# Local attention in a five-block model: the value product with channels on the partitions, and the query norm inside the mask-and-maximum op

## The chip, the cores and the metric

The kernel runs on one core of one Trainium2 chip, as one program in fp32. The metric is device time in microseconds (us). Three runs of the kernel before gave 1146.81, 1147.2 and 1147.84, median 1147.2. Engine names: PE is the matmul engine (PEld its weight loads), DVE the vector engine, ACT the scalar engine, POOL the GpSimd engine, SP the queue that issues nearly all DMAs.

## The reference

The input is x of shape (4, 512, 128): 4 batches, 512 positions, 128 channels. Six blocks follow each other, each with a residual sum around a layer norm: a gated feed-forward, a 16-head attention with a position bias, the same feed-forward again, then twice a block of two local-attention layers with a recurrence between. What the change touches is the local attention, of which there are 2 blocks x 2 layers x 4 batches = 16 calls. Cut to what matters:

```python
qkv = h @ wqkv                       # 8 heads of 64 channels
q = l2norm(q) * qs ; k = l2norm(k) * ksc
q, k = rotary_xpos(q, k)             # q*cos*scale + rotate_half(q)*sin*scale, and so on
# windows of 64 queries; keys: the window before and the same window (128 keys)
sim = einsum('bhwid,bhwjd->bhwij', bq * 8.0, bk)
sim = where((i < j) | (i > j + 64) | (j == -1), -max, sim)
attn = softmax(sim)
out = einsum('bhwij,bhwjd->bhwid', attn, bv)
x = x + out @ wo
x = x + feed_forward(x)              # layer norm, 128 -> 2*341, a * gelu(g), -> 128
```

## The kernel before

**A planner writes the order.** The kernel does not issue instructions as its functions run. Each call on an engine is recorded as an `Op` with a guessed cost and a due time (`plan.vt`); `Plan.plan` (lines 179 to 265) then places the ops one by one, as each engine comes free and its inputs and buffers are there, the one with the earliest due time first; `emit` issues them in that order and `pin` fixes it, so that every engine works through one fixed list. All instructions therefore carry line 318, where the recorder calls the engine. Costs, due-time steps (`STEP`, `TURN`), and a few biases are constants at the head of the file. Buffers are slots that the planner hands out: 8 PSUM banks "psS", 33 "pair" buffers of which each can serve as two "half" ones, 24 "small" tiles, 8 "va" tiles for values.

**Stages.** The first feed-forward and the 16-head attention (head pair by head pair, batch by batch) fill the first 420 us or so; the feed-forward again overlaps with its end; the local blocks follow, the four batches shifted against each other and interleaved by the planner. From the first to the last product with `wqkv` it is 423 to 1075 us.

**One call of `local_attention` (lines 684 to 875)** treats 4 tiles of 128 positions, so there are 64 tiles in all. A tile passes these functions, several steps apart (`behind`, line 869), while other tiles and other batches are between them:

- `rotate` (690): two products with `wqkv` for q and k; ACT squares them; DVE multiplies by the cos and sin tables into `u` and `w`; POOL adds halves of the squares, DVE sums them, three small ACT ops give the inverse norms `rn` of 8 query and 8 key heads; POOL adds the rotated halves and multiplies all 1024 columns of `u` by `rn` (line 721).
- `values` (726): the product for v, copied by ACT into `va` of 8 x 65 columns; column 64 of each head holds ones, so that the value product also gives the softmax sum.
- `turn` (734): 4 PE transposes turn the queries, ACT copies them; the keys are turned by a DVE block transpose and DMAs.
- `soften` (771): 16 small products give scores for 8 heads x 128 keys. One DVE op per head (lines 790 to 794) adds the mask, negates, writes the result and its minimum `mx`. ACT takes exp of the first 4 heads with `mx` as bias; for the other 4 heads POOL subtracts `mx` (line 798) and ACT takes one exp.
- `turn_back` (804): 8 PE transposes turn the undivided exponentials, ACT copies them to `pT`; DMAs bring the values of the window before into `vm`.
- `weigh` (822): the value product with positions on the partitions: 16 products, weights `pT` (64 columns of positions), moving `val` (65 columns). DVE takes the reciprocal of the sums (line 838) and multiplies 4 heads at a time out of PSUM (line 839).
- `turn_outputs` (844): 4 PE transposes bring channels onto the partitions, ACT copies.
- `project` (853): 4 products with `wo`, two DVE adds into the residual `h`.

Of the kernel before, what the change touches and what calls it, by code (L numbers as in the profile page):

```python
# [9 lines left out]
ALU = mybir.AluOpType  # L10
# [25 lines left out]
KEYS = 2 * WIN  # L36
DX = DH + 1
QK_SCALE = 8.0
NEG = -1.0e30

# [13 lines left out]
PAIRS = 33  # L54
STEP, TURN = 3.368, 10.272
ATTN, LATE, LAG, LATER = 28.945, 383.972, 3.899, 11.219

# [63 lines left out]
class Plan:  # L121
# [3 lines left out]

    LATENCY, HORIZON, SWITCH, TABLE = 0.07, 52.328, 0.1, 1.28
    IDLE, COLD, FIRST = 2.5, 8.0, 6

    TAIL = {"tensor": 0.16, "vector": 0.085, "scalar": 0.115, "gpsimd": 0.05}
    MODE_BIAS, TABLE_BIAS = 15.205, 15.629  # L130

# [167 lines left out]
class Recorder:  # L299
# [36 lines left out]
    def cost(self, name, outs, ins, kw, n):  # L336

        if name == "dma_start":
            return 0.55
        if name == "matmul":  # L340
            return max(0.22, ins[1].size() / 597.0)
        if name == "transpose":
            return 0.12 if self.engine == "tensor" else 0.62
        if n is None:
            n = max(v.size() for v in (ins if name == "tensor_reduce" else outs) or outs)
        if self.engine == "vector":
            if name == "tensor_tensor_scan":
                return 1.2
            psum = any(v.tile.kind == "S" for v in ins)
            lo, hi = (outs + ins)[0].region()[0]  # L350
            if name == "tensor_tensor_reduce":
                return 0.078 + 0.00104 * n
            inside = len(ins) > 1 and n > 256 and not psum
            return 0.064 + 0.00104 * n + 0.09 * (hi - lo <= 64) + 0.06 * (len(ins) > 2) + 0.3 * inside
        if self.engine == "scalar":
            if name == "copy":
                return 0.04 + 0.00083 * n
            wide = len(ins) > 1 or any(v.tile.kind != "S" for v in ins)
            return 0.05 + 0.00083 * n + 0.09 * wide + 0.06 * ("accum_out" in kw)
        if name == "memset":  # L360
            return 0.1 + 0.0008 * n
        return 0.145 + 0.0022 * n
# [66 lines left out]
def tile_macaron(ctx: ExitStack, tc: tile.TileContext, i: dict, out: bass.AP):  # L429
# [6 lines left out]
    def real(name, shape, pool=pool):  # L436
# [4 lines left out]
            "S": [real(f"psS{n}", [P, T], psum) for n in range(8)],  # L441
            "small": [real(f"small{n}", [P, 2 * H1]) for n in range(24)],
            "va": [real(f"va{n}", [P, H1, DX]) for n in range(8)],
            "via": [real(f"via{n}", [P, 2 * T], dram) for n in range(8)],
# [239 lines left out]
    def local_attention(l, h):  # L684
        wqkv, wo = wqkv_sb[l], wo1_sb[l]
        cs, sn = cos_sb[l], sin_sb[l]
        half = DH // 2
        us, qTs, kTs, vas, vms, es, pTs, os_, oTs = ({} for _ in range(9))

        def rotate(t):  # L690
# [27 lines left out]
            for lo, hi in ((slice(0, half), slice(half, DH)), (slice(half, DH), slice(0, half))):  # L718
                pool_.tensor_tensor(u4[..., lo], u4[..., lo], w4[..., hi], ALU.add, n=INNER)
            u3 = u.rearrange("p (h d) -> p h d", d=DH)  # L720
            pool_.tensor_tensor(
                u3, u3, rn.unsqueeze(2).to_broadcast([P, 2 * H1, DH]), ALU.mult, cost=1.87
            )
            us[t] = u

        def values(t):
# [3 lines left out]
            )  # L730
            va = vas[t] = plan.tile("va", [P, H1, DX])
            act.copy(va[:, :, :DH], pv)

# [37 lines left out]
        def soften(t):  # L771
# [26 lines left out]
            pool_.tensor_tensor(  # L798
                rest, rest, mx[:, BIASED:].unsqueeze(2).to_broadcast([P, H1 - BIASED, KEYS]), ALU.subtract
            )  # L800
            act.activation(rest, rest, AF.Exp, scale=-1.0)
            es[t] = e

        def turn_back(t):


            vm = vms[t] = plan.tile("half", [P, H1, DX])
            dma.dma_start(out=vm[64:128], in_=vas[t][0:64])
# [252 lines left out]
    w_h = cload("w_h", [D, D], i["L1_attn_Wh"])  # L1061
    for va in memory.slots["va"]:
        pool_.memset(plan.fixed(va, [P, H1, DX])[:, :, DH:], 1.0)


# [13 lines left out]
def _constants():  # L1079
# [92 lines left out]
```

## Time and profile before

| what | value |
|---|---|
| median of three runs | 1147.2 us |
| the profiled execution: span from first to last instruction | 1146.1 us |
| median less span (what lies around it) | 1.1 us |
| granted PE clock | 1.00 of full speed |
| instructions: PE, DVE, ACT, POOL | 9036, 2891, 1948, 575 |
| local blocks | from about 420 us to the end |
| PE transposes in all | 1488 that read a "pair" buffer, 1024 of them in the local attention |

How to read it: the page gives busy time of each engine and a strip of 40 slices with busy tenths; a busy PE is one that has a matmul in its pipeline. Further views give the chain of work that ended last, groups of instructions of one shape with count, busy time and mean duration, busy time by stretches of time, and a timeline. A group's mean duration is from an instruction's start to its end; consecutive instructions on PE, DVE and ACT overlap, so that what one costs its engine is the distance from start to start, which the timeline tells. An fp32 product of PE is recorded as two instructions, a transpose as one.

### The profile page before, as it was taken

How to read it: one execution, taken by the hardware profiler on the slowest of the kernel's cores; microseconds unless marked ns; L12 is line 12 of the kernel's file. 1: busy time of each engine (PE TensorE's matmuls, PEld its weight loads, DVE VectorE, ACT ScalarE, POOL GpSimd, SP SyncE). 2: the span in 40 equal slices, each digit the busy share in tenths (PEclk: the TensorE clock that was granted, in tenths of full speed). 3: DMA queues.
4: the chain of work that ended last, by engine and by line, in shares of the span. 5: the costliest groups of instructions: out<-in, count | busy, mean ns of one | idle time of the engine just before them, and what ended most of it. 6: DMA issues, size and time to landing. Idle time of an engine off the chain costs nothing.

```text
span 1146.1 us, 26884 instructions
## 1 busy us (share of the span) xinstructions
PE 1117.0 (97%) x9036; PEld 688.4 (60%) x9036; DVE 911.9 (80%) x2891; ACT 877.0 (77%) x1948; POOL 762.7 (67%) x575
## 2 busy tenths in 40 slices
PE   7999999999999999999999999999999999999997
PEld 3455656566655545557667666764457766666673
DVE  4787787868778779989788788867999978878863
ACT  5987777867787667878786788788887777777764
POOL 3675655656569459979776677523999867777610
PEclk9999999999999999999999999999999999999999
DMA  4379799797979744523432332300333423322310
GB/s 126 125 232 306 211 261 264 207 274 206 299 211 309 199 115 127 161 84 106 120 96 68 93 102 76 85 1 1 98 114 102 115 77 101 98 84 67 98 38 19
DMA packets 131613, 157.01 MB, mean 137 GB/s; under 512 B 15034, under 2 KB 101732, under 8 KB 131476
## 3 DMA queue, kind: packets, MB, share of 16 engines
q1 hardware_dynamic: 131188, 155.21, 46.4%
q8 instruction: 73, 1.20, 0.5%
q14 instruction: 64, 0.52, 0.2%
q10 hardware_dynamic: 288, 0.08, 0.0%
HBM read 78.39 MB, written 64.02 MB: 124 GB/s over the span
## 4 chain that ended last, share of the span: by engine, by line
PE 70%; DVE 13%; ACT 9%; issue 3%; POOL 2%; DMA 1%; SPq 0%; DVEq 0%; ACTq 0%; POOLq 0%
PE psS L318 70%; DVE pair L318 12%; ACT pair L318 7%; POOL pair L318 2%; DVE small L318 1%; ACT small L318 1%; DMA pair<-via 1%; ACT L288 1%; ACT va L318 1%; SPq L318 0%; DMA via<-pair 0%; DMA pair<-in_x_dram 0%; DVE xT L318 0%; DVEq L318 0%; ACTq L318 0%
## 5 line engine op out<-in xcount | busy, mean ns | idle before, releaser
L318 POOL TENSOR_TENSOR pair<-pair,small 128x1024 f32<-128x1024 f32 (+1 forms) x256 | 430.9, 1704 | 203.6 <-DVE small L318 127.7
L318 PE MATMUL psS<-pair,pair 64*64 64x128 f32 (+4 forms) x4544 | 372.5, 300 | 3.2 <-DVE small L318 1.3
L318 ACT ACTIVATE pair<-pair,small 128x128 f32<-128x128 f32 (+1 forms) x512 | 266.5, 553 | 91.7 <-DVE small L318 77.1
L318 PEld LDWEIGHTS psS<-pair,pair 128*64 128x64 f32 (+2 forms) x4544 | 252.6, 140 | 101.5 <-issue 31.3
L318 ACT COPY pair<-psS 128x512 f32<-128x512 f32 (+1 forms) x470 | 254.6, 593 | 63.5 <-PE psS L318 59.0
L318 POOL TENSOR_TENSOR pair<-pair,pair 128x512 f32<-128x512 f32 x166 | 215.2, 1309 | 109.1 <-ACT pair L318 66.8
L318 PEld LDWEIGHTS psS<-ident,pair 128*128 128x128 f32 x1488 | 171.2, 141 | 92.5 <-issue 69.9
L318 PE MATMUL psS<-ident,pair 128*128 128x128 f32 x1488 | 200.0, 275 | 9.2 <-DMA pair<-in_x_dram 5.5
L318 DVE CUSTOM_DVE_ANT_0 pair<-psS,pair 128x512 f32<-128x512 f32 x256 | 164.8, 679 | 37.1 <-PE psS L318 36.3
L318 PE MATMUL psS<-wqkv,pair 128*128 128x512 f32 x384 | 182.2, 598 | 3.4 <-DVE pair L318 3.0
L318 DVE STREAM_TRANSPOSE pair<-pair 128x512 f32<-128x512 f32 x208 | 142.8, 697 | 18.9 <-POOL pair L318 18.0
L318 POOL TENSOR_TENSOR pair<-pair 128x512 f32<-128x512 f32 x82 | 102.9, 1256 | 55.8 <-ACT pair L318 54.7
L318 PE MATMUL psS<-pair,w 128*128 128x512 f32 (+2 forms) x288 | 130.2, 595 | 0.4 <-POOL pair L318 0.2
L318 ACT ACTIVATE pair<-pair 128x512 f32<-128x512 f32 x152 | 94.5, 629 | 35.6 <-DVE pair L318 26.4
L318 DVE CUSTOM_DVE_ANT_0 pair<-psS,mask 128x128 f32<-128x128 f32 x512 | 113.9, 284 | 6.2 <-PE psS L318 4.8
L318 PE MATMUL psS<-pair 64*128 64x512 f32 x512 | 117.7, 601 | 0.0
L318 PEld LDWEIGHTS psS<-wqkv,pair 128*128 128x128 f32 x384 | 68.6, 190 | 74.6 <-issue 50.1
L318 DVE TENSOR_TENSOR pair<-psS,cos 128x512 f32<-128x512 f32 x128 | 87.2, 681 | 18.5 <-ACT pair L318 15.1
L318 DVE TENSOR_TENSOR pair<-psS,sin 128x512 f32<-128x512 f32 x128 | 87.2, 681 | 15.2 <-ACT pair L318 14.6
L318 ACT ACTIVATE pair<-psS 128x512 f32<-128x512 f32 x144 | 82.0, 596 | 18.6 <-PE psS L318 10.3
L318 PEld LDWEIGHTS psS<-pair,w 128*128 128x128 f32 (+2 forms) x288 | 50.7, 182 | 62.8 <-issue 49.5
L318 PEld LDWEIGHTS psS<-pair 64*128 64x128 f32 x512 | 48.5, 186 | 58.5 <-issue 42.0
(73 smaller groups left out, 1191.3 us busy)
## 6 DMA issues: line engine op xcount, KB each, us to landing
via<-pair SPq DMA_DIRECT2D x72, 512.0 KB, 3.8
pair<-via SPq DMA_DIRECT2D x288, 128.0 KB, 3.8
via<-pair SPq DMA_DIRECT2D x64, 256.0 KB, 2.1
pair<-via SPq DMA_DIRECT2D x256, 64.0 KB, 2.1
pair<-va SPq DMA_DIRECT2D x112, 130.0 KB, 2.3
table<-tdram SPq DMA_DIRECT2D x16, 511.5 KB, 7.2
pair<-table SPq DMA_DIRECT2D x16, 448.0 KB, 4.6
pair<-pair SPq DMA_DIRECT2D x48, 128.0 KB, 2.0
```

Of the source, the lines that this page charges most:

```text
L288: self.nc.scalar.add_instruction(mybir.InstLoadActFuncSet(name=self.nc.get_next_instruction_name(), engine=mybir.EngineType.Activation, ac ...
L318: real(*[a.resolve() if isinstance(a, View) else a for a in args], **{k: a.resolve() if isinstance(a, View) else a for k, a in kw.items()},)
```

## The change

1. `weigh` swaps the roles of its operands: `val` (64 columns, one head) becomes the weights and `pT` (64 positions) the moving operand, the two heads of a pair on the two halves of the columns. The result `po` has channels on the partitions, as `project` needs it, and ACT copies it to `oTs`. `turn_outputs` is gone, and with it one step of the pipeline (NT + 8 becomes NT + 7, `project` 7 behind).
2. Since channels are on the partitions the sum can no longer be divided out there. So `soften` divides: the four biased exps also write their sums (`accum_out`), DVE sums the other four heads in one reduce, two reciprocals follow, and POOL multiplies the 1024 columns in two halves before they are turned. The column of ones in `va` is gone.
3. The query half of line 721 is gone: POOL scales the 512 key columns only. The query norm is the `scale` operand (one column per head) of the mask-and-minimum op of DVE, which had the constant -1; the sign moves into the query table, and the mask is +1e30 in place of -1e30. Heads are stored in the order of parity.
4. Constants of the planner: costs of three kinds of ops, 32 "small" tiles for 24, and its due-time steps and biases.

The core of the diff:

```diff
-STEP, TURN = 3.368, 10.272
-ATTN, LATE, LAG, LATER = 28.945, 383.972, 3.899, 11.219
+STEP, TURN = 3.332, 10.933
+ATTN, LATE, LAG, LATER = 29.952, 380.996, 3.898, 11.327
...
-            wide = len(ins) > 1 or any(v.tile.kind != "S" for v in ins)
-            return 0.05 + 0.00083 * n + 0.09 * wide + 0.06 * ("accum_out" in kw)
+            wide = any(v.tile.kind != "S" for v in ins[:1])
+            return 0.05 + 0.00083 * n + 0.042 * wide + 0.093 * (len(ins) > 1) + 0.093 * ("accum_out" in kw)
...
-            u3 = u.rearrange("p (h d) -> p h d", d=DH)
+            keys = u[:, INNER:].rearrange("p (h d) -> p h d", d=DH)
             pool_.tensor_tensor(
-                u3, u3, rn.unsqueeze(2).to_broadcast([P, 2 * H1, DH]), ALU.mult, cost=1.87
+                keys, keys, rn[:, H1:].unsqueeze(2).to_broadcast([P, H1, DH]), ALU.mult, cost=0.98
             )
...
-            for hd in range(H1):
+            sm = plan.tile("small", [P, H1])
+            rn = rns.pop(t)
+
+            for n in range(H1):
+                j, pr = divmod(n, H1 // 2)
+                hd = 2 * pr + j
                 dve.tensor_tensor_reduce(
-                    out=e[:, hd, :], in0=sc[hd // (H1 // 2)][:, hd % (H1 // 2), :], in1=mask,
-                    scale=-1.0, scalar=BIG, op0=ALU.add, op1=ALU.min, accum_out=mx[:, hd : hd + 1],
-                )
-            for hd in range(BIASED):
-                act.activation(e[:, hd, :], e[:, hd, :], AF.Exp, bias=mx[:, hd : hd + 1], scale=-1.0)
-            rest = e[:, BIASED:, :]
+                    out=e[:, n, :], in0=sc[j][:, pr, :], in1=mask,
+                    scale=rn[:, hd : hd + 1], scalar=BIG, op0=ALU.add, op1=ALU.min,
+                    accum_out=mx[:, n : n + 1],
+                )
+            for n in range(BIASED):
+                act.activation(
+                    e[:, n, :], e[:, n, :], AF.Exp, bias=mx[:, n : n + 1], scale=-1.0,
+                    accum_out=sm[:, n : n + 1],
+                )
...
-            act.activation(rest, rest, AF.Exp, scale=-1.0)
+            act.activation(e[:, rest, :], e[:, rest, :], AF.Exp, scale=-1.0)
+            dve.tensor_reduce(sm[:, rest], e[:, rest, :], AX.X, ALU.add)
+            for part in (slice(0, H1 // 2), slice(H1 // 2, H1)):
+                dve.reciprocal(sm[:, part], sm[:, part])
+                pool_.tensor_tensor(
+                    e[:, part, :], e[:, part, :],
+                    sm[:, part].unsqueeze(2).to_broadcast([P, H1 // 2, KEYS]), ALU.mult, cost=0.98,
+                )
...
         def weigh(t):
-            o = os_[t] = plan.tile("half", [P, H1, DH])
-            for r in range(2):
-                po = plan.tile("S", [P, H1 // 2, DX])
-                with plan.bundle(0.52, "col"):
-                    for hh in range(H1 // 2):
-                        hd = r * (H1 // 2) + hh
-                        for blk, val in enumerate((vm, va)):
+            po = plan.tile("S", [P, H1 // 2, P])
+            with plan.bundle(1.0, "col"):
+                for pr in range(H1 // 2):
+                    for blk, val in enumerate((vm, va)):
+                        c = slice(blk * WIN, (blk + 1) * WIN)
+                        for j in range(2):
                             pe.matmul(
-                                po[blk * WIN : (blk + 1) * WIN, hh, :],
-                                lhsT=pT[:, (hd % 2) * (H1 // 2) + hd // 2, blk * WIN : (blk + 1) * WIN],
-                                rhs=val[:, hd, :], start=True, stop=True,
+                                po[j * DH : (j + 1) * DH, pr, c], lhsT=val[:, 2 * pr + j, :],
+                                rhs=pT[:, j * (H1 // 2) + pr, c], start=True, stop=True,
                             )
-                rc = plan.tile("small", [P, H1 // 2, 1])
-                dve.reciprocal(rc, po[:, :, DH:], n=4)
-                dve.tensor_tensor(
-                    o[:, r * (H1 // 2) : (r + 1) * (H1 // 2), :], po[:, :, :DH],
-                    rc.to_broadcast([P, H1 // 2, DH]), ALU.mult,
-                )
-
-        def turn_outputs(t):
-            of = os_.pop(t).rearrange("p h d -> p (h d)")
-            ptp = plan.tile("S", [P, H1 // 2, P])
-            with plan.bundle(0.44):
-                for pr in range(H1 // 2):
-                    pe.transpose(ptp[:, pr, :], of[:, pr * P : (pr + 1) * P], ident)
             oTs[t] = plan.tile("half", [P, H1 // 2, P])
-            act.copy(oTs[t], ptp)
+            act.copy(oTs[t], po)
...
-        order = (project, turn_outputs, turn_back, turn, values, rotate, soften, weigh)
-        behind = {values: 0, rotate: 0, turn: 2, soften: 3, turn_back: 5, weigh: 6,
-                  turn_outputs: 7, project: 8}
-        for k in range(NT + 8):
+        order = (project, turn_back, turn, values, rotate, soften, weigh)
+        behind = {values: 0, rotate: 0, turn: 2, soften: 3, turn_back: 5, weigh: 6, project: 7}
+        for k in range(NT + 7):
...
-    mask = np.where(mask, f4(0.0), f4(NEG)).astype(f4)
+    mask = np.where(mask, f4(0.0), f4(FAR)).astype(f4)
...
-        q, k = QK_SCALE * a * scale, a / scale
+        q, k = -QK_SCALE * a * scale, a / scale
```

More of the change, by code (lines that the diff above doesn't have):

```diff
@@ L36 @@
 KEYS = 2 * WIN
-DX = DH + 1
 QK_SCALE = 8.0
-NEG = -1.0e30
+FAR = 1.0e30
 BIASED = 4
@@ L121 @@
 class Plan:
-    LATENCY, HORIZON, SWITCH, TABLE = 0.07, 52.328, 0.1, 1.28
+    LATENCY, HORIZON, SWITCH, TABLE = 0.07, 52.449, 0.1, 1.28
     IDLE, COLD, FIRST = 2.5, 8.0, 6
     TAIL = {"tensor": 0.16, "vector": 0.085, "scalar": 0.115, "gpsimd": 0.05}
-    MODE_BIAS, TABLE_BIAS = 15.205, 15.629
+    MODE_BIAS, TABLE_BIAS = 14.843, 16.541
     def __init__(self, tc, memory):
@@ L441, in tile_macaron @@
             "S": [real(f"psS{n}", [P, T], psum) for n in range(8)],
-            "small": [real(f"small{n}", [P, 2 * H1]) for n in range(24)],
-            "va": [real(f"va{n}", [P, H1, DX]) for n in range(8)],
+            "small": [real(f"small{n}", [P, 2 * H1]) for n in range(32)],
+            "va": [real(f"va{n}", [P, H1, DH]) for n in range(8)],
             "via": [real(f"via{n}", [P, 2 * T], dram) for n in range(8)],
@@ L687, in local_attention @@
         half = DH // 2
-        us, qTs, kTs, vas, vms, es, pTs, os_, oTs = ({} for _ in range(9))
+        us, rns, qTs, kTs, vas, vms, es, pTs, oTs = ({} for _ in range(9))
         def rotate(t):
@@ L719, in rotate @@
                 pool_.tensor_tensor(u4[..., lo], u4[..., lo], w4[..., hi], ALU.add, n=INNER)
-            u3 = u.rearrange("p (h d) -> p h d", d=DH)
+            keys = u[:, INNER:].rearrange("p (h d) -> p h d", d=DH)
             pool_.tensor_tensor(
-                u3, u3, rn.unsqueeze(2).to_broadcast([P, 2 * H1, DH]), ALU.mult, cost=1.87
+                keys, keys, rn[:, H1:].unsqueeze(2).to_broadcast([P, H1, DH]), ALU.mult, cost=0.98
             )
-            us[t] = u
+            us[t], rns[t] = u, rn
         def values(t):
@@ L730, in values @@
             )
-            va = vas[t] = plan.tile("va", [P, H1, DX])
-            act.copy(va[:, :, :DH], pv)
+            va = vas[t] = plan.tile("va", [P, H1, DH])
+            act.copy(va, pv)
         def turn(t):
@@ L788, in soften @@
             mx = plan.tile("small", [P, H1])
-            for hd in range(H1):
+            sm = plan.tile("small", [P, H1])
[3 more added lines that the diff above has]
+                hd = 2 * pr + j
                 dve.tensor_tensor_reduce(
-                    out=e[:, hd, :], in0=sc[hd // (H1 // 2)][:, hd % (H1 // 2), :], in1=mask,
-                    scale=-1.0, scalar=BIG, op0=ALU.add, op1=ALU.min, accum_out=mx[:, hd : hd + 1],
-                )
-            for hd in range(BIASED):
-                act.activation(e[:, hd, :], e[:, hd, :], AF.Exp, bias=mx[:, hd : hd + 1], scale=-1.0)
-            rest = e[:, BIASED:, :]
+                    out=e[:, n, :], in0=sc[j][:, pr, :], in1=mask,
+                    scale=rn[:, hd : hd + 1], scalar=BIG, op0=ALU.add, op1=ALU.min,
+                    accum_out=mx[:, n : n + 1],
+                )
+            for n in range(BIASED):
[3 more added lines that the diff above has]
+                )
+            rest = slice(BIASED, H1)
+            over = [P, H1 - BIASED, KEYS]
             pool_.tensor_tensor(
-                rest, rest, mx[:, BIASED:].unsqueeze(2).to_broadcast([P, H1 - BIASED, KEYS]), ALU.subtract
-            )
-            act.activation(rest, rest, AF.Exp, scale=-1.0)
+                e[:, rest, :], e[:, rest, :], mx[:, rest].unsqueeze(2).to_broadcast(over),
+                ALU.subtract, cost=0.07 + 0.0018 * (H1 - BIASED) * KEYS,
+            )
+            act.activation(e[:, rest, :], e[:, rest, :], AF.Exp, scale=-1.0)
[6 more added lines that the diff above has]
+                )
             es[t] = e
         def turn_back(t):
-            vm = vms[t] = plan.tile("half", [P, H1, DX])
+            vm = vms[t] = plan.tile("half", [P, H1, DH])
             dma.dma_start(out=vm[64:128], in_=vas[t][0:64])
@@ L1061, in tile_macaron @@
     w_h = cload("w_h", [D, D], i["L1_attn_Wh"])
-    for va in memory.slots["va"]:
-        pool_.memset(plan.fixed(va, [P, H1, DX])[:, :, DH:], 1.0)
     for b in range(B):
```

## Prediction

> **What bounds the kernel now.** I read the page first: its busy line, strip and chain.
>
> ```profile
> PE 1117.0 (97%) x9036; PEld 688.4 (60%) x9036; DVE 911.9 (80%) x2891; ACT 877.0 (77%) x1948; POOL 762.7 (67%) x575
> ...
> POOL 3675655656569459979776677523999867777610
> ...
> PE 70%; DVE 13%; ACT 9%; issue 3%; POOL 2%; DMA 1%; SPq 0%; DVEq 0%; ACTq 0%; POOLq 0%
> ```
>
> PE is busy nearly always and holds 70% of the chain that ended last, POOL 2%. So PE's work counts first. But the strip shows POOL at 9 tenths or more twice, where the local blocks begin and where their second half begins. An average of 67% hides that. So I cut the local stage into stretches (columns: length, busy PE, PEld, DVE, ACT, POOL):
>
> ```profile
> 420.00:560.00 140.00, 136.18 (x1194) 83.64 (x1191) 127.74 (x394) 110.83 (x255) 125.44 (x98) 1.00 0.38 115
> 560.00:720.00 160.00, 158.96 (x1644) 107.45 (x1644) 130.64 (x476) 125.16 (x276) 115.50 (x92) 1.00 0.31 89
> 720.00:810.00 90.00, 88.05 (x646) 52.15 (x642) 67.35 (x193) 72.12 (x129) 35.21 (x33) 1.00 0.08 23
> 810.00:920.00 110.00, 104.72 (x1077) 69.52 (x1076) 102.21 (x350) 90.75 (x215) 102.87 (x81) 1.00 0.39 114
> 920.00:1080.00 160.00, 157.98 (x1527) 103.68 (x1527) 130.18 (x459) 121.13 (x271) 115.12 (x93) 1.00 0.30 88
> ```
>
> In 560–720 and 920–1080 PE is at 99% and POOL at 72%: PE's stretches. In 420–560 and 810–920 PE is at 97 and 95%, DVE at 91 and 93%, POOL at 90 and 94%: three engines are near full. How much delay PE can take I got by setting the trace beside the program's order and taking, for each group of transposes, its start less the end of the last writer of its input. The median is 8.4 us in 560–720 and in 920–1080, but 0.9 us in 810–920 and 3.2 in 420–560. In PE's stretches a late operand is swallowed, at 810–920 it isn't.
>
> The durations come from groups of one shape (busy us, then mean ns of one) and from the timeline:
>
> ```profile
> L318 POOL TENSOR_TENSOR pair<-pair,small 128x1024 f32<-128x1024 f32 x192 | 365.1, 1922 | 169.9 <-DVE small L318 104.8 <-ACT small L318 34.5 <-PE psS L318 21.3
> L318 POOL TENSOR_TENSOR pair<-pair,small 128x512 f32<-128x512 f32 x64 | 66.9, 1048 | 33.7 <-DVE small L318 22.9 <-PE psS L318 5.5 <-DMA pair<-va 5.2
> L318 DVE TENSOR_TENSOR pair<-psS,small 128x256 f32<-128x256 f32 x128 | 49.9, 418 | 1.0
> L318 DVE RECIPROCAL small<-psS 128x4 f32<-128x4 f32 x128 | 17.4, 166 | 1.9 <-PE psS L318 1.6
> L318 DVE TENSOR_REDUCE small<-pair 128x16 f32<-128x512 f32 x64 | 42.9, 670 | 10.8 <-POOL pair L318 10.6
> L318 DVE SCALAR_TENSOR_TENSOR pair<-psS,xT 128x512 f32<-128x512 f32 x24 | 16.3, 678 | 7.0 <-PE psS L318 5.6 <-POOL pair L318 1.2
> L318 DVE SCALAR_TENSOR_TENSOR xT<-psS,vecs,pair 128x512 f32<-128x512 f32 x8 | 6.0, 750 | 4.7 <-PE psS L318 4.5
> ```
>
> ```profile
> 645.70 1.47 PE L318 MATMUL psS<-ident,pair 128*128 128x128 f32 x12
> ...
> 656.38 1.91 PE L318 MATMUL psS<-ident,pair 128*128 128x128 f32 x16
> ```
>
> **The change part by part.**
>
> PE. 64 tiles lose 4 transposes each, 256. Twelve in a row take 1.47 us, sixteen 1.91: four cost 0.44, one 0.11. That is 64 x 0.44 = 28 us. The page's mean of 275 ns for one is start to end and overlaps with the next; it is not what goes. (The Trainium skill, "TensorE: Matmul & The Clock Gate", Part 4: PE-mode transpose, gives about 275 ns for a 128x128 transpose in one kernel's context; by that the 256 would be an estimated 70 us. The trace agrees on the duration and shows a spacing of 0.11, so the sum doesn't use it.) The value product stays at 16 products per tile in two column halves, 64 moving columns for 65: 1/65 of its 67 us busy, 1 us. By the built order PE changes between full, row and column packing 208 times, before 192; at a change the spacing grows by some 93 ns (a transpose before a score product starts the next after 202 ns, not 109), +1.5 us. PE: -27.5 us.
>
> POOL. The norm op shrinks from 1024 to 512 columns: the rows give 1.92 - 1.05 = 0.87 less. Two divisions of 512 columns come: 2 x 1.05. Net +1.23 per tile, 79 us in all, on an engine that has 494 us of work in the 660 us from 420 to 1080. The divisions fall with `soften` (11, 15, 6, 12 and then 20 tiles in the stretches, by the count of the subtract), the saving with `rotate` (15, 16, 3, 14, 16).
>
> POOL's new wait. Between a tile's subtract and its first division lie ACT's exp (0.63), the reduce (0.67) and a reciprocal (0.16), with the hand-overs some 1.7 us. In the built order of POOL nothing stands between the two for 9 tiles, one op for 24, two for 18, more for 13. An op takes 1.05 to 1.3, so POOL stands still for about 1.7, 0.6 and 0: 9 x 1.7 + 24 x 0.6 = 30 us, 0.46 per tile. Behind the held division are the next tile's `rotate` ops, and behind these DVE's reduce and key turn. DVE or ACT queues can make it worse; it can't be below zero. Bounds 0 and, were each chain 3 us long, about 100 us.
>
> DVE. It loses 128 evacuations and 128 reciprocals out of PSUM (49.9 + 17.4 = 67 us busy) and gains 64 reduces (43) and 128 small reciprocals (0.16 each, 20): -4. The 512 mask ops get a scale per partition, and no row shows this op with one. The nearest rows bound it: another op of 512 columns out of PSUM takes 678 without and 750 with such a column; so 0 to 72 ns each, 0 to 37 us; below zero nothing speaks for it. I take 60, nearer the pair of rows: +31. DVE +27 in all, 0.4 per tile. The norm itself is there long before the scores, so it adds no wait.
>
> ACT. 256 exps write their sums. In the 16-head attention such a read starts and 0.10 us later the next exp starts (258.35 to 258.45); its own row is 189 ns. So +24 us, at most 48; ACT's 558 us from 420 on become 582, cover enough. The copy behind `turn_outputs` becomes the copy behind `weigh`: same shape, same count. DMAs stay 112 for the values, 128 KB for 130, off the path.
>
> What goes as a stall: the pipeline loses one step (transposes, copy), about 1.2 us of a tile's way, and gains about 3 in `soften`. In the interleaved stages PE has other tiles to work on; in the last 60 us it works on feed-forward products. I cost both at nothing; uncovered, in the last call alone, it is some 2 us.
>
> **The sum.** In 810–920 POOL's demand becomes 102.9 + 12 x 2.1 - 14 x 0.87 + 12 x 0.46 = 121 in 110: 11 too much. After 920 POOL has a quarter of its time free and PE has reserve, so part of the backlog is worked off there; I take 7 us of lengthening (bounds 0 and 16), and the 8 tiles projected there don't bring their 3.5. In 420–560 it is 125.4 + 11 x 2.1 - 15 x 0.87 + 11 x 0.46 = 140.5 in 140, where it has 10% idle now: 3 us (0 to 12). In the other stretches POOL comes to 87% or so, and PE keeps its saving. 1146.1 - 27.5 + 7 + 3.5 + 3 = 1132.1; with the 1.1 us that lie between span and median, **1133**.
>
> **The rivals.**
>
> - *The whole saving.* All queues stay ahead of PE and its 27.5 us come out: 1120. For it: POOL's 2% of the chain, and PE's reserve of 3 us and more outside 810–920. Against: POOL at 94% there.
> - *DVE takes the second half's start.* If the scale costs its 72 ns, DVE's 102.2 us in 810–920 get 12 x 0.5 on top and reach 108 of 110, while POOL's held divisions wait behind them on DVE's reduce: another 7 us, 1140. For it: DVE leads the pieces of the chain in 805–840. Against: a DVE that is late only there.
> - *Slower: the in-order division.* POOL can't go past a division whose sum isn't there, and the rotations of the next tiles stand behind it. POOL's work from 420 to 1080 would be 494 + 79 = 573; about 40 us of the hole at 720–810, where the recurrence gives it nothing to do, can't be used. So 620 us are usable now, and 47 us of waits, 0.75 us per tile, bring back the old length. At 1.0 us per tile (64 us) the stage is some 16 us longer: 1163. For it: the order with no or one op between for 33 of 64 tiles, and subtracts that today, in half the cases, have their exp within 0.05 us, so little is spare. Against: my 0.46 per tile.
> - *Nothing to see.* Gain and waits balance, 1147. That the change doesn't do what it says I exclude: the built order has 1232 transposes of "pair" buffers for 1488.
>
> **Chances.** Forecast (1126 to 1144) 0.42; whole saving (1115 to 1126) 0.18; DVE (1136 to 1148) 0.12, a third of it within the bound; slower (1150 to 1175) 0.24; balance 0.04. About 0.2% is what a measurement of this kernel can tell from no change. Faster: 0.42 + 0.18 + 0.08 = 0.68; same 0.04 + 0.04 = 0.08; slower 0.24. The range runs from inside the whole saving, 1117, to the nearer half of the slower case, 1158.
>
> **What would show it.** PE: transposes 1232 and busy time near 1090. POOL busy near 840, idle before divisions put down to "DVE small"; if that idle is far over 30 us, the slower case holds. Mean of the mask op: 284 before, 344 if the scale costs 60. In the windows, the steady stretches should be shorter and the two starts not. Wrong would be: PE idle in the steady stretches too, where POOL then must be over 95%.

## The result, and the profile after

| | before | after |
|---|---|---|
| median of 17 runs each, us | 1147.77 | 1149.65 |
| ratio to before | | 1.0016 [1.0009, 1.0024] |
| profiled execution: span, us | 1146.1 | 1149.4 |
| busy PE, DVE, ACT, POOL, us | 1117.0, 911.9, 877.0, 762.7 | 1100.2, 937.4, 896.3, 834.9 |

The kernel got 1.9 us longer, which lies within the 0.2% named in the prediction, where 1133 and "faster" were forecast. PE has less to do and the kernel isn't shorter. The page after, its busy line, two rows of the strip and its chain:

```profile
PE 1100.2 (96%) x8780; PEld 661.5 (58%) x8780; DVE 937.4 (82%) x2827; ACT 896.3 (78%) x2204; POOL 834.9 (73%) x695
...
DVE  4787787778779779999899798777999988898863
...
POOL 3675665657569458999898797643899998988750
...
PE 4%; DVE 1%; POOL 0%; issue 0%; ACT 0%; DVEq 0%
```

The chain breaks off after 5% of the span and is no help. The stretches are (columns: length, busy PE, PEld, DVE, ACT, POOL, PE's clock, DMA share, GB/s):

```profile
420.00:560.00 140.00, 134.10 (x1157) 80.19 (x1154) 130.51 (x384) 111.66 (x292) 126.62 (x111) 1.00 0.35 106
560.00:720.00 160.00, 153.75 (x1539) 99.38 (x1538) 140.20 (x483) 129.01 (x352) 139.18 (x131) 1.00 0.32 93
720.00:810.00 90.00, 85.19 (x636) 48.36 (x635) 67.90 (x158) 73.01 (x138) 43.16 (x42) 0.98 0.10 29
810.00:920.00 110.00, 99.19 (x985) 61.74 (x984) 105.57 (x333) 90.34 (x247) 103.12 (x94) 1.00 0.33 99
920.00:1080.00 160.00, 153.98 (x1476) 98.89 (x1474) 137.53 (x456) 129.22 (x342) 140.64 (x133) 0.99 0.32 93
```

Beside the same stretches before: in 560–720 and 920–1080 PE fell from 158.96 and 157.98 to 153.75 and 153.98, while DVE rose from 130.64 and 130.18 to 140.20 and 137.53 (86 to 88%) and POOL from 115 to 140. Below 90% no other engine looks full in them, and yet PE, 99% busy before, now stands still where the forecast had it undisturbed. PE's idle time from 420 us on, summed from the trace, is 37.7 us for 16.5 before.

The groups whose prices the forecast had to estimate (busy us, mean ns, then the idle time just before them and what ended it), and the mask op as it was before:

```profile
L317 POOL TENSOR_TENSOR pair<-pair,small 128x512 f32<-128x512 f32 x256 | 268.7, 1064 | 72.1 <-DVE small L317 32.8 <-ACT small L317 19.6 <-PE psS L317 9.9
...
L317 DVE CUSTOM_DVE_ANT_0 pair<-psS,mask,small 128x128 f32<-128x128 f32 x512 | 145.9, 344 | 10.5 <-PE psS L317 6.4 <-ACT pair L317 3.5
...
L317 DVE TENSOR_REDUCE small<-pair 128x4 f32<-128x512 f32 x64 | 43.3, 676 | 3.8 <-ACT pair L317 3.4
```

```profile
L318 DVE CUSTOM_DVE_ANT_0 pair<-psS,mask 128x128 f32<-128x128 f32 x512 | 113.9, 284 | 6.2 <-PE psS L318 4.8 <-issue 0.5 <-ACT pair L318 0.5
```

The mask op went from 284 to 344 ns, from start to start from 211 to 271: 60 ns x 512 = 31 us of DVE. The 256 ops of POOL in the first row are the subtracts, the norms of the keys and both divisions of each tile; with the trace set beside the program's order, POOL's waits come to 25.0 us before the first divisions and 6.2 before the second ones (forecast 30). So each price was near enough. What failed is what they were taken to cost.

### The profile page after: what moved, and what is told of

Its sections match the earlier page's. It is cut to its first block, busy times and chain, and to the rows that moved or that the text cites. A ratio compares the mean times of both kernels' runs of the same rounds, so it can differ in the third digit from the quotient of the medians.

```text
span 1149.4 us, 26716 instructions
## 1 busy us (share of the span) xinstructions
PE 1100.2 (96%) x8780; PEld 661.5 (58%) x8780; DVE 937.4 (82%) x2827; ACT 896.3 (78%) x2204; POOL 834.9 (73%) x695
## 5 line engine op out<-in xcount | busy, mean ns | idle before, releaser
L317 POOL TENSOR_TENSOR pair<-pair,small 128x512 f32<-128x512 f32 (+1 forms) x384 | 508.0, 1343 | 205.8 <-DVE small L317 121.0
L317 ACT ACTIVATE pair<-pair,small 128x128 f32<-128x128 f32 (+1 forms) x512 | 281.8, 552 | 88.8 <-DVE small L317 70.7
L317 PEld LDWEIGHTS psS<-pair,pair 128*64 128x64 f32 (+2 forms) x4532 | 242.3, 141 | 102.3 <-issue 32.8
L317 PEld LDWEIGHTS psS<-ident,pair 128*128 128x128 f32 x1232 | 143.4, 142 | 96.9 <-issue 63.0
L317 PE MATMUL psS<-ident,pair 128*128 128x128 f32 x1232 | 172.4, 276 | 13.3 <-DMA pair<-in_x_dram 6.0
L317 DVE STREAM_TRANSPOSE pair<-pair 128x512 f32<-128x512 f32 x208 | 143.8, 700 | 23.9 <-POOL pair L317 21.8
L317 DVE CUSTOM_DVE_ANT_0 pair<-psS,mask,small 128x128 f32<-128x128 f32 x512 | 145.9, 344 | 10.5 <-PE psS L317 6.4
L317 PE MATMUL psS<-pair 64*128 64x512 f32 (+2 forms) x524 | 121.0, 596 | 0.0
L317 ACT ACTIVATION_READ_ACCUMULATOR pair<-pair,small 128x1 f32 x512 | 96.6, 189 | 0.0
L317 DVE TENSOR_REDUCE small<-pair 128x16 f32<-128x512 f32 (+1 forms) x128 | 86.0, 675 | 11.3 <-POOL pair L317 7.4
```

What stands on the lines that cost most here:

```text
L317: real(*[a.resolve() if isinstance(a, View) else a for a in args], **{k: a.resolve() if isinstance(a, View) else a for k, a in kw.items()},)
```

## The experiments

Where "after's order" is said, all engines work through the instructions of after in its order, apart from what the edit changes or adds. The others are ordered by the planner anew. The runs of before beside them had medians of 1147.2 to 1147.6 us.

**First set: which of the two new burdens is it?** After's order; POOL's divisions on one column per head, 4 elements for 512 (e1), the mask op's scale a constant (e2), both (e3):

```diff
-    e[:, part, :], e[:, part, :], sm[:, part].unsqueeze(2).to_broadcast([P, H1 // 2, KEYS]), ALU.mult,
+    e[:, part, 0:1], e[:, part, 0:1], sm[:, part].unsqueeze(2), ALU.mult,       # e1, e3
-    scale=rn[:, hd : hd + 1], scalar=BIG,
+    scale=1.0, scalar=BIG,                                                      # e2, e3
```

> The changed kernel in its own order on every engine, but each division on POOL touches one column per head (4 elements) and no longer 512: left out is the division of the rest. The wait for the sums stays, the 128 x 1.05 us of POOL work go down to some 0.1 us each. POOL theory (the new POOL work makes keys and probabilities late and eats PE's saving): 1120 to 1126, PE idle in the local stage back to some 16 us. DVE theory (the mask op's extra 60 ns, 31 us in all, is what delays PE): no lower than 1140. Order theory (the fixed order fits badly, whatever the durations): no lower than 1140.

> The changed kernel in its own order, but the mask op gets the constant 1.0 as scale and not the column of norms: left out is the query norm. DVE loses 512 x 60 ns = 31 us, POOL keeps its work. DVE theory: 1125 to 1135. POOL theory: 1143 to 1149, since the divisions still hold POOL. Order theory: within 3 us of the changed kernel.

> Both of the above at once, order unchanged: left out are the query norm and most of the division. If POOL and DVE together eat the saving, here all of it is back: 1119 to 1122 (PE's 27.5 us). If this stays above 1135, neither is the cause and the order or the longer way of a tile is.

Measured: e1 1139.45 (0.9930 [0.9916, 0.9945]), e2 1127.12 (0.9833 [0.9809, 0.9858]), e3 1120.24 (0.9763 [0.9747, 0.9780]). The page of e3, and its first long stretch:

```profile
PE 1089.4 (97%) x8780; PEld 661.1 (59%) x8780; DVE 900.5 (81%) x2827; ACT 892.1 (80%) x2204; POOL 728.4 (65%) x695
```

```profile
560.00:720.00 160.00, 159.36 (x1644) 104.09 (x1642) 139.30 (x504) 134.54 (x365) 117.73 (x137) 1.00 0.33 98
```

e1 lies just under the 1140 that the DVE theory allowed. Without both burdens PE is full again (159.36 of 160) and the whole saving of PE comes out: 27 us, and PE's busy time falls by as much (1117.0 to 1089.4). So the transposes are worth what was said. Of the 29 us that take it back, the column's 31 us of DVE carry 22.5 (1149.65 - 1127.12), and 108 us of POOL work only 10.2. Mind the DVE share of e3, 139.30 in this stretch: as high as in after, since more work passes in the same time (PE's instructions are 1644 for 1539). A busy share doesn't show which engine sets the pace.

e2 and after have one list on PE, so the starts of its instructions can be compared place by place. After is level with e2 until 420 us, and late by 3.5 us at e2's 560, 8.5 at 700, 14.1 at 720, 13.6 at 810, 15.7 at 920 and 23.9 at 1080. So the column costs in the long stretches above all, and the step of 5.6 between 700 and 720 is one event, which comes up again below.

**The column alone, in before's order** (the constant -1 read from a column that holds -1):

```diff
-    scale=-1.0, scalar=BIG, op0=ALU.add, op1=ALU.min,
+    scale=neg1, scalar=BIG, op0=ALU.add, op1=ALU.min,
```

> The kernel before, in its own order on every engine, with one edit: the mask op reads its scale -1 from a column of -1 and not from a constant. It computes the same; DVE gets 512 x 60 ns = 31 us more. DVE theory: 1162 to 1175, though DVE is busy only 80% of the span. If what counts is an engine's busy share and PE's reserve swallows the rest, as my prediction had it: 1148 to 1156.

Measured: 1171.95 (1.0214 [1.0199, 1.0229]), +24.7 us for 31 us of DVE. Its mask op and two stretches:

```profile
L318 DVE CUSTOM_DVE_ANT_0 pair<-psS,mask,neg 128x128 f32<-128x128 f32 x512 | 144.8, 345 | 5.9 <-PE psS L318 4.4 <-issue 0.5 <-ACT pair L318 0.5
```

```profile
560.00:720.00 160.00, 154.77 (x1527) 103.17 (x1526) 134.51 (x457) 121.34 (x271) 112.42 (x91) 1.00 0.29 85
...
920.00:1080.00 160.00, 152.98 (x1546) 100.95 (x1539) 132.86 (x456) 115.79 (x264) 112.87 (x92) 1.00 0.29 83
```

Nothing but 60 ns on each of 512 ops, no division, no POOL wait, DVE only 84% busy, and PE loses 4 to 5 us in each long stretch. Where PE's time goes, the trace tells when it is set beside the program's order. The table puts each idle time of PE after 420 us down to what came last for the group of products or transposes behind it: the writer of an operand, or the last reader of the PSUM bank that the group writes next (waits for DMAs and inside groups are left out). The last two rows are the prediction's reserve, the time from the last writer of the transposes' input to their start, in the two long stretches.

| | before | e10 | after | e2 | e3 |
|---|---|---|---|---|---|
| PE idle for an operand, us | 10.0 | 14.6 | 27.4 | 17.0 | 12.2 |
| PE idle for a bank, us | 6.3 | 18.1 | 7.1 | 2.5 | 2.7 |
| reserve of transposes, median, 560–720 | 8.4 | 8.3 | 5.9 | 6.5 | 7.5 |
| the same, 920–1080 | 8.9 | 8.3 | 2.9 | 4.6 | 5.9 |

In before's order it is mostly the banks, 11.8 us of the 16.4 that e10 adds. The inputs of the transposes keep their reserve, but from the last reader of a bank to PE's next write into it there was little to begin with: a median of 2.3 us over all groups in 560–720, a quarter under 1.5, and 2.0 and 1.1 in e10. In the changed kernel it is the operands: 17.4 us more idle time for them, 0.8 for banks. There the reserve itself has shrunk, to 5.9 and 2.9 us.

PE's clock is a small part. The granted clock was 1.00 in the profiled runs of before, e10 and e3, and 0.996 in that of after, which has two stretches of 3.4 us at half clock ahead of its last 4 us: 3.4 us at most. e10 has none and is 24.7 us longer.

**Each half of the change alone.** e4 is before with the query norm's part; e5 is after without it (POOL scales 1024 columns, the constant -1); e11 is e5 with POOL's norm planned at the cost of 512 columns, which brings its order nearer to after's.

> The kernel before with the query norm alone moved into the mask op (POOL 0.87 us per tile less, DVE 0.48 more; output transposes and division as before). POOL theory: 1140 to 1146, POOL is relieved at the two full stretches. DVE theory: 1150 to 1158. Its planned order is its own, so a few us either way are not told apart.

> The changed kernel without the query-norm part: POOL scales all 1024 columns again (+0.87 us per tile, 56 us), the mask op has the constant -1 again (DVE 31 us less). DVE theory: 1127 to 1134, a little above the run with the constant scale (1127.1), since 128 us of POOL's divisions taken away were worth 10 and 7 us. POOL theory: 1150 or more, POOL has 56 us more than in the changed kernel. Planned anew, so a few us are not told apart.

> The value product with channels on the partitions, without the query-norm part (mask op with the constant -1, POOL scales 1024 columns), planned with the cost of 512 columns so that the order stays close to the changed kernel's: 345 of 5014 places differ on PE. DVE theory: 1128 to 1138, the constant-scale run's 1127 and a few us for 56 us more on POOL; it would beat both kernels. POOL theory, or the order as in the same kernel planned with true costs (1176): over 1150.

Measured: e4 1179.85 (1.0281 [1.0266, 1.0297]), e5 1176.38 (1.0260 [1.0236, 1.0284]), e11 1175.79 (1.0249 [1.0223, 1.0275]). e5's long stretches:

```profile
560.00:720.00 160.00, 153.05 (x1555) 98.60 (x1553) 129.32 (x463) 126.37 (x336) 151.41 (x130) 0.99 0.30 89
...
920.00:1080.00 160.00, 152.43 (x1518) 97.00 (x1518) 129.78 (x454) 127.58 (x339) 154.01 (x132) 1.00 0.31 91
```

Either half alone makes the kernel 29 to 33 us longer, apparently for different reasons: e4 pays DVE's column and has no use for the 53 us that POOL is spared (busy 709.6), though it lies above both of its expected ranges, so its new order may add to it; e5 puts POOL at 95%. Together they come to 2. The norm's part is what makes room for the divisions, at a price on DVE.

**The order as such.** e6: the planner's cost of the mask op gets the 60 ns (`+ 0.06 * (len(ins) > 2)`). e7: reduce and divisions become a step of their own, one step after `soften`. e8: after with before's due-time constants; e9: before with after's.

> The changed kernel with one number of the planner changed: the mask op with a scale column is planned 0.06 us dearer, as it is on the chip. All instructions are the same, only their order differs. Misfit theory (the 60 ns hurt because the fixed order was made without them): 1125 to 1136. Queue theory (DVE's longer work in the middle of its list delays what stands behind, in any order): 1144 to 1152.

> The changed kernel with the reduce, the reciprocals and the divisions recorded one pipeline step later, so that POOL has other work between the subtract and the division. POOL waits some 28 us before divisions in the changed kernel. If the held division is a main cause: 1135 to 1143. If it is not (DVE theory): 1146 to 1152, with the idle time before divisions under 15 us all the same.

> The changed kernel with the due-time steps and biases of the kernel before: the same instructions in another order. It tells how much an order alone is worth. DVE theory: 1145 to 1160, since the 31 us on DVE stay. If the changed order is simply a bad one: under 1138.

> The kernel before with the due-time steps and biases of the changed one: same instructions, another order. It tells how much of any difference here can be due to a new order: by the changed kernel with the old constants (13 us slower) 1150 to 1170.

Measured: e6 1147.11 (0.9996 [0.9987, 1.0006]), e7 1161.21 (1.0123 [1.0106, 1.0139]), e8 1162.51 (1.0130 [1.0115, 1.0145]), e9 1154.09 (1.0059 [1.0042, 1.0076]). Constants alone move before by 7 us and after by 13. So runs with an order of their own (e4, e5, e7) can't be read to less than some 10 us, and that e7's later division is worse isn't shown by it: its 1161, above both expected ranges, lies among the orders of after. e6 speaks against the misfit theory: planned with the true cost, the kernel gains 2.5 us, where that theory wanted 14 or more. The size of a single burden is to be read from runs in one order only.

**Is it the mask op's place, or DVE's time anywhere?** e12, after's order: the reduce replaced by a 4-element op (the division of four heads is then by one exponential).

```diff
-    dve.tensor_reduce(sm[:, rest], e[:, rest, :], AX.X, ALU.add)
+    dve.tensor_scalar(sm[:, rest], e[:, rest, WIN], 1.0, None, ALU.add, cost=...)
```

> The changed kernel in its own order, scale column kept, but the DVE reduce over 4 x 128 probabilities becomes a DVE op on 4 elements (1 + one of them): left out is the sum, so the division is by something else. That takes 64 x some 0.55 us = 35 us from DVE at another place than the mask op. If DVE time in general is what eats the saving: 1122 to 1132. If it is the scale column itself (a port, its wait for the norm): 1144 to 1150.

Measured: 1149.04 (1.0010 [1.0000, 1.0019]): no gain, and I took it as proof that only the mask op's place counts. The next four runs add two DVE ops per tile to e2, in after's order: behind the 4th and the 8th mask op, reading the mask table in SBUF (e13) or the score bank in PSUM (e14); behind each sine product, reading its PSUM bank (e15); both behind the reduce, reading the mask table (e16).

```diff
+    nc.vector.tensor_tensor_reduce(out=scr, in0=<mask table, or the bank>, in1=<mask table>, scale=1.0,
+        scalar=BIG, op0=ALU.add, op1=ALU.min, accum_out=col)
```

> The kernel after with the mask op's scale as the constant 1.0 (which leaves out the query norm; it took 1127.1 us), its order, and two more DVE ops of 128 columns per tile, one behind the fourth and one behind the eighth mask op. They read only the mask table and write a scratch tile: DVE is held some 0.42 us per tile (27 us in all) at the place where the column held it 0.48, but no score bank is read by the added ops and each score bank's last reader is at most one added op late. If DVE's in-order time at this place is what counts: 1127 + 22 x 0.42/0.48 = 1146 (1142 to 1150). If the score banks that are held are what counts: well below that, 1128 to 1136. If the later start of the exps counts: also low, since the exps of the first four heads keep their time: 1128 to 1136.

> As the run with two more DVE ops that read the mask table, but the added ops read the score bank that the four mask ops ahead of them have read, so each bank is held one op longer. If the held banks count: above its sibling by most of the cost, 1142 to 1150. If DVE's time in order counts: the same as its sibling within 3 us. If the exps' start counts: low, 1128 to 1136, as its sibling.

> The same two added ops per tile on the kernel with the constant scale, but behind the sine products of rotate, where they read the bank with q or k. If any DVE time that holds a PSUM bank counts: 1140 to 1150. If what counts is the place of the mask op alone: 1127 to 1133.

> The same two added ops per tile on the kernel with the constant scale, both behind the reduce that sums the four unbiased heads, reading the mask table only. The reduce's own time was worth nothing when it was taken away, so if DVE time counts by place: 1127 to 1132. If 27 us more of DVE cost the same wherever they are put: 1142 to 1150.

Measured: e13 1178.28 (1.0265 [1.0252, 1.0279]), e14 1146.06 (0.9983 [0.9974, 0.9993]), e15 1154.46 (1.0051 [1.0035, 1.0067]), e16 1180.80 (1.0289 [1.0275, 1.0302]). The two that touch no bank are by far the worst, which none of the theories allows. The added ops' rows in e13 and in e14 tell why:

```profile
L479 DVE CUSTOM_DVE_ANT_0 scr<-mask 128x128 f32<-128x128 f32 x128 | 75.7, 591 | 0.0
```

```profile
L479 DVE CUSTOM_DVE_ANT_0 scr<-psS,mask 128x128 f32<-128x128 f32 x128 | 36.4, 285 | 0.0
```

The same op takes 591 ns with both operands in SBUF, 285 with one in PSUM. Two of them in e13's timeline (start, duration), DVE and then POOL:

```profile
600.60 1.16 DVE L479 CUSTOM_DVE_ANT_0 scr<-mask 128x128 f32<-128x128 f32 x1
...
659.83 0.29 DVE L479 CUSTOM_DVE_ANT_0 scr<-mask 128x128 f32<-128x128 f32 x1
```

```profile
600.57 1.04 POOL L317 TENSOR_TENSOR pair<-pair,small 128x512 f32<-128x512 f32 x1 [0.27 <-DVE small L317]
...
660.05 1.04 POOL L317 TENSOR_TENSOR pair<-pair,small 128x512 f32<-128x512 f32 x1 [4.31 <-PE psS L317]
```

The first starts 0.03 us behind an op of POOL, which ends at 601.61; it ends 0.15 us after that. The second starts 0.22 us ahead of POOL's op and takes its 0.29. Of the 128 added ops of e13, 113 found an op of POOL running when they started; all of these ended within 0.22 us of its end (median 522 ns, up to 2005), and the 15 others took 284 (median). In e14, where one operand is in PSUM, 116 found POOL running and none took over 289. So DVE waits here for POOL, inside its op, and the whole in-order queue of DVE with it. The 4-element op of e12 had done the same:

```profile
L317 DVE TENSOR_SCALAR small<-pair 128x4 f32<-128x4 f32 x64 | 36.3, 568 | 3.3 <-ACT pair L317 3.1
```

568 ns for 4 elements: up to the start of DVE's next op the 64 ops sum to 33.6 us, the reduces of after to 41.2. e12 had taken 8 us off DVE and not 35, and its "proof" was void.

(The Trainium skill, "SBUF — State Buffer", section "SBUF: two separate sides", says that DVE and GpSimd share a pair of ports that is locked for a whole instruction, and that a DVE op takes it in a two-port mode or with two inputs in SBUF, against a GpSimd op that reads SBUF. The runs agree: two SBUF inputs waited, a PSUM input didn't. The page would have warned of e13, e16 and, as to a two-port mode, of e12, though the runs don't tell which mode its op was in.)

The changed kernel itself holds such a wait. Here are two ops of DVE of one form, with both operands in SBUF; the last of four ops of POOL that follow each other without a gap from 721.19 on; PE's next product with its idle time; and the stretch behind it (the 0.50 is PE's clock):

```profile
721.72 4.71 DVE L317 SCALAR_TENSOR_TENSOR pair<-pair,xT 64x512 f32<-64x512 f32 x1
...
727.05 0.69 DVE L317 SCALAR_TENSOR_TENSOR pair<-pair,xT 64x512 f32<-64x512 f32 x1
```

```profile
724.64 1.24 POOL L317 TENSOR_TENSOR pair<-pair 128x512 f32<-128x512 f32 x1
```

```profile
728.67 1.93 PE L317 MATMUL psS<-pair,w 128*128 128x512 f32 x3 [3.68 <-DVE pair L317]
```

```profile
729.70:733.10 3.40, 3.40 (x6) 0.87 (x5) 2.89 (x6) 2.92 (x9) 2.24 (x3) 0.50 0.00 0
```

DVE's op takes 4.71 us for 0.69, and PE stands still for 3.68. In the profiled executions of e1, e2 and e3 no op of DVE takes over 2.4 us; e14 and e15 have this one too (4.84 and 4.75), e18 has another (4.88 at 874.1). 3.68 us and half of the 3.4 at half clock make 5.4, the step between e2 and after at this place. So a quarter of e2's 22.5 us hangs on one op that met a row of POOL's, and the rates in the next table are no smooth law.

**The test done properly.** e18, after's order: still a reduce, but over every 32nd key only.

```diff
-    dve.tensor_reduce(sm[:, rest], e[:, rest, :], AX.X, ALU.add)
+    dve.tensor_reduce(sm[:, rest], e[:, rest, ::32], AX.X, ALU.add, cost=...)
```

> The kernel after in its own order, where the reduce that sums the four unbiased heads adds 4 keys of each head instead of 128 (so the division of these heads is by a partial sum). Unlike the 4-element op that was put there before, which waited for a running POOL op (568 ns mean, 456 ns from start to start), a reduce showed no such wait, so this takes some 0.45 to 0.5 us per tile off DVE, 29 to 32 us in all, away from the mask op. If a microsecond of DVE in the local blocks costs 0.7 to 1 us of the whole wherever it stands: 1149.6 - 0.75 x 30 = 1127 (1119 to 1132). If only the mask op's place is dear: 1147 to 1150.

Measured: 1137.51 (0.9916 [0.9902, 0.9931]).

```profile
L317 DVE TENSOR_REDUCE small<-pair 128x4 f32<-128x16 f32 x64 | 10.9, 171 | 3.9 <-ACT pair L317 3.8
```

32 us less of DVE at the reduce (598 to 93 ns from start to start, by 64) gain 12.1 us. All steps of one order together, DVE's time taken from start to start:

| run | against | DVE time | whole | per us of DVE |
|---|---|---|---|---|
| e2, column gone | after | -31 | -22.5 | 0.73 |
| e10, column in before | before | +31 | +24.7 | 0.80 |
| e14, at the mask op | e2 | +27.0 | +18.9 | 0.70 |
| e15, at the sine product | e2 | +26.4 | +27.3 | 1.03 |
| e13, at the mask op, with waits | e2 | +66.9 | +51.2 | 0.77 |
| e16, at the reduce, with waits | e2 | +62.7 | +53.7 | 0.86 |
| e18, reduce cut | after | -32 | -12.1 | 0.38 |

DVE's time costs at each of three places, so "only the mask op's place" is wrong; but e18 gave half of what the plain rule expected (0.75, time 1127), so a microsecond isn't worth the same everywhere. e14 against e13, as far as a rate without waits can be set beside one with them, shows no extra for a bank held 0.2 us longer. Why the reduce's time is worth less stays open.

**The norm where it costs DVE nothing.** e17: the query norm as scale column of the exps; all 8 heads take a biased exp with a sum, POOL's subtract and DVE's reduce go, the mask op has a constant.

```diff
+    dve.scalar_tensor_tensor(mx3, mx3, -1.0, rq, op0=ALU.mult, op1=ALU.mult)
-    for n in range(BIASED):
-        act.activation(e[:, n, :], e[:, n, :], AF.Exp, bias=mx[:, n : n + 1], scale=-1.0,
+    for n in range(H1):
+        act.activation(e[:, n, :], e[:, n, :], AF.Exp, bias=mx[:, n : n + 1], scale=rn[:, hd : hd + 1],
                        accum_out=sm[:, n : n + 1])
-    pool_.tensor_tensor(...subtract...); act.activation(...Exp...); dve.tensor_reduce(...)
```

> The kernel after with the query norm as the scale column of the exps in place of the mask op (correct output, own order): all 8 heads take a biased exp that writes its sum, so POOL's subtract (67 us) and DVE's reduce (38 us) are gone, the mask op has a constant again (31 us), and one small DVE op per tile makes the biases (6 us). DVE some 63 us less than after, POOL 67 less plus its waits, ACT 4 x 0.385 - 0.53 = 1.0 us per tile more, 64 us, to about 960 of 1120. If DVE's time is what counts and ACT has room: the whole PE saving, 1120 (1112 to 1130). If only the mask op's place counts: 1127, give or take 10 for another order. If ACT takes DVE's part as the engine that sets the pace: 1140 to 1165.

Measured: 1216.63 (1.0602 [1.0588, 1.0615]), the worst of all, with DVE at 72%:

```profile
PE 1119.6 (92%) x8780; PEld 671.1 (55%) x8780; DVE 882.2 (72%) x2827; ACT 1002.0 (82%) x2652; POOL 773.1 (64%) x631
```

```profile
L317 ACT ACTIVATE pair<-pair,small,small 128x128 f32<-128x128 f32 x512 | 245.3, 483 | 21.1 <-DVE small L317 20.8
```

The third case came, ACT as the new pacer, beyond the 1165 allowed for it: an exp with a second column takes 483 ns for 390, from start to start 385 for 292, so with the 93 for its sum a tile's exps need 8 x 0.477 = 3.8 us in one block for 2.1. 49 of PE's 86 us of idle time after 420 end on ACT's tiles, and the granted clock was 0.98, 0.996 in after; by my estimate from these two that is 19 of its 1217 us at most. Its order is new as well, and the planner costs an exp with two columns like one with one, so not all of it need be ACT. (The Trainium skill, "ScalarE: Activation LUTs", section "What ACT_TABLE_LOAD costs", gives some 93 ns for each pointer operand of an ACTIVATE; the runs agree to the nanosecond. My expectation had left it out, 48 us of ACT.) So there is no version here that beats before by more than the 0.2%; the nearest is e6.

## Why the prediction was wrong, point by point

- **PE -27.5: right.** e3 lies 27 us below before, and PE's busy time there 27.6.
- **POOL +79, waits of 30: right in size** (busy 834.9 for some 840, waits 31). The 13.5 us put down for POOL at the two starts (7 + 3.5 + 3) stand against 10.2 that the divisions' width cost (e1), and in other places: by PE's starts, after falls behind e1 by 1.3 us in the two starts, 420–560 and 810–920, and by 4.5 at the one op at 721.7.
- **ACT +24**: busy +19.3; no run took it away, but e3 has it and the whole saving.
- **DVE +27: priced right and costed at nothing.** This is the step that failed. The mask op is at 344 as said; the sum has no term for it. It measured 22.5 us (e2; 5.6 of them the op at 721.7) and 24.7 (e10).
- **"In PE's stretches (560–720 and 920–1080) a late operand is swallowed": wrong, and the reason for the missing term.** The 8.4 us were the median reserve of the transposes' inputs, in the order of before. PE also waits for its outputs, the PSUM banks that DVE and ACT empty, and there a quarter of the groups had under 1.5 us; this is what e10 ran into. And the changed kernel doesn't have the reserve of before: 5.9 and 2.9 us are left of it, and most of PE's added idle time is for late operands. I measured the kind of wait with most to spare, and in the kernel that was about to change. Adding measured terms: 1120.2 (e3) + 22.5 + 10.2 = 1152.9, of which 3 overlap, and 1149.65 came; that the op at 721.7 counts in both terms fits the overlap.
- **The rivals.** "DVE takes the second half's start" had the right engine and even the argument against it ("a DVE that is late only there"), but was priced at 7 us at one place; DVE's price fell due in the long stretches above all. "Slower: the in-order division" needed 47 us of waits to bring back the old length; they came to 31. "Nothing to see" gave the right time, but with its balance between gain and POOL's waits; in the runs DVE's column took most, so its time was right by luck.
- **"What would show it"** named PE idle in the steady stretches "where POOL then must be over 95%". PE was idle there with POOL at 87 and 88%: a test that looked at one suspect.

Still open: why DVE, 83 to 88% busy in the long stretches, sets the pace at 0.4 to 1.0 us per microsecond. The in-order queues of four engines, which hand each tile round several times, make that likely, since no engine can fill its gaps with work that stands behind a waiting op; no run took the order away to show it.

## What to carry to other kernels

When an engine at 80% is given more work, don't ask whether it has idle time, ask how long the engine that sets the pace has until it waits for it, for its inputs and for the buffers that it writes, at the lower quartile and not at the median of the kindest group; and expect the change itself to use some of it up. A cheap test before a change of this sort is to give the op its new operand with an old value (e10): one line in the order that is there, and it would have told 25 us. And look at the duration of what you put in as a light substitute, and at the longest ops of each form; a 4-element op of 568 ns is a wait, and so is one of 4.71 us among its likes of 0.69.

## What the runs showed of the hardware

- A scale read from a column costs this DVE op 60 ns (284 to 344; 211 to 271 from start to start), and ACT's exp 93 (292 to 385 from start to start). The read of an accumulated sum costs ACT another 93.
- A DVE op with both operands in SBUF waits inside its own duration while POOL works, up to 2.0 us in e13 and through four ops of POOL, 4.71 us, in after, and shows no idle time before it: its row is only longer (591 for 285). A 4-element op from SBUF to SBUF did the same (e12, 568 ns). The reduces, reciprocals and block transposes of this kernel showed no such spread (reduces of 512 columns 636 to 691 ns, block transposes 660 to 714).
- A change of due-time constants alone moved the kernels by 7 and 13 us (e9, e8), more than most single edits.
